# Layer 3's coupling: the first half kept as the input of its first Gelu, the last additions on three engines

## The chip, the cores and the metric

The kernel runs on one core of a Trainium2 chip. The metric is device time in microseconds of one execution of the whole program; the median of several executions is given with the lowest and the highest. Beside it stands one execution recorded by the hardware profiler, whose rows are used for everything inside the kernel.

The engines are named as in the profile: PE is TensorE (matmuls), PEld its weight loads, ACT is ScalarE, DVE is VectorE, POOL is GpSimd, SP the engine that issues the DMAs here.

## The reference, cut to what matters

The program runs four layers, each with an attention-like part and a feed-forward part. Only the end of the last layer is touched. There, a state x of 4096 rows by 128 features goes three times through a coupling. Its coefficient comes from a small net on x and from a context net on the mean of x:

```
for cycle in 0, 1, 2:
    h = gelu(x @ c1 + cb1)          # 128 -> 128
    h = gelu(h @ c2 + cb2)          # -> 64
    h = gelu(h @ c3 + cb3)          # -> 32
    c = base + c2s * tanh((h @ c4 + cb4) / 2)   # one number for each row
    x = x + c * twist(x)            # twist is a fixed signed permutation of features
out = residual + x
```

The lines are the mathematics as the kernel computes it: base comes from the context net and holds one number for each batch entry, c2s is a constant of the layer. The matrix twist, applied twice, gives minus the identity, so that several cycles together are a*x + b*twist(x) with two numbers a and b for each row.

## The kernel before, in words

The 4096 rows are eight blocks of 512. A block lies with its features on the partitions, as the tile xT[i] of 128 x 512; two batch entries of 256 rows make a block. Blocks 0 to 3 are the first half, 4 to 7 the second (HALVES). The residual lies with rows on the partitions, as X[i].

The first cycle's c1 of blocks 0 to 3 is done inside the last layer's attention, by attended (line 1285), where two single PSUM banks are to be had. After attention, bank gives one of four PSUM buffers, and tp has four more, named tw.

Each step of the coupling is a small function, and each works on one half. first (from line 1333) multiplies a block by c1 and runs the Gelu on ACT from PSUM (L1339). second joins two blocks in one bank (L1347), third joins four (L1355). fourth multiplies by c4 for each block; ACT's tanh (L1401) gives the coefficient, repeated over all 128 partitions; DVE multiplies it by the constant and the twisted block (L1402); POOL and DVE in turn add that to xT (L1403). twists makes the twisted block on PE, in tw, and lets DVE add the part of base at once (L1391, two instructions for each block). columns_of computes the same coefficients once more with rows on the partitions (cd on PE, L1362 on ACT, L1366 on DVE), and keeps the products a and b up.

In the last cycle xT of the first half is not updated. finish_first forms a*x + b*twist(x) from the tile with rows on the partitions, xn, for all four blocks: m is the b part (L1435), in four instructions for each block, y is scaled by a (L1436), and both are added to the residual (L1440, L1441). POOL makes m and y for blocks 0 and 1, DVE for blocks 2 and 3; DVE does all additions. The second half is different: rest_in (L1416) adds its xT to the residual through PE, turn_second twists it on PE (tx), and finish_second adds the twisted block times the coefficient (L1457), on DVE. SP then issues each output block's DMA.

The order of everything after attention is written out by hand under a manual schedule of PE, ACT, DVE and POOL: each engine runs its instructions in the order of the calls, and waits only for what an instruction reads and for the buffer that it writes to. The two halves alternate, so that PE works on one half while ACT and DVE are busy with the other.

Of the kernel before, what the change touches and what calls it, by code (L numbers as in the profile page):

```python
# [10 lines left out]
F32 = mybir.dt.float32  # L11
# [3 lines left out]
ALU = mybir.AluOpType  # L15
# [40 lines left out]
def program(ctx: ExitStack, tc: tile.TileContext, x, consts, consts0, rows, pk0, w0s, w0e, pk1, pk1i, pk2, pk3, out):  # L56
# [1201 lines left out]
    with tc.tile_pool(name="l3w", bufs=1) as wp:  # L1258
# [11 lines left out]
        with banks(2, 3), tc.tile_pool(name="l3a", bufs=2) as sp:  # L1270
            gx = wp.tile([P, B], F32, tag="gx", name="gx")

            def means():
                yield from norm_steps(fp, (NBLK - 1,), 3, kept)
                for i in range(NBLK):
                    nc.vector.tensor_reduce(
                        gx[:, 2 * i : 2 * i + 2], xT[i].rearrange("p (b s) -> p b s", b=2), AX.X, ALU.add
                    )
                    yield
                nc.vector.tensor_scalar(gx, gx, 1.0 / S, None, ALU.mult)  # L1280
                yield

            h1 = {}

            def attended(s, gap, cT):


                ahead = {(16, 5): (0, 1), (17, 0): (2,), (17, 1): (3,)}
                for i in ahead.get((s, gap), ()):
                    ps = bank(f"c1_{i}_0")  # L1290
                    mm(ps, W3["c1"], xT[i])
                    h1[i] = wp.tile([P, 512], F32, tag=f"c1_{i}", name=f"c1_{i}_0")
                    nc.scalar.activation(h1[i], ps, AF.Gelu, bias=W3["cb1"])  # L1293
                if s in (14, 15) and gap in (1, 2, 4):
                    i = (s - 14) * 3 + gap // 2
                    po = bank(f"po3_{i}")
                    for t in range(NT):
                        ts_ = slice(t * P, (t + 1) * P)
                        mm(po[:, ts_], cT[i][:, ts_], W3["wo"])
                    xf = X[i].rearrange("p t d -> p (t d)")  # L1300
                    nc.vector.tensor_tensor(xf, xf, po, ALU.add)

            cTs = attention(sp, wp, range(NBLK), W3, 3, means(), attended)

        with banks(4, 0), tc.tile_pool(name="l3t", bufs=4, space=PSUM, reuse_waits="tile") as tp, \
# [24 lines left out]
            def first(hf, cyc, ns):  # L1333
                for n in ns:
                    i = HALVES[hf][n]
                    ps = bank(f"c1_{i}_{cyc}")
                    mm(ps, W3["c1"], xT[i])
                    h1[i] = sp.tile([P, 512], F32, tag="c1", name=f"c1_{i}_{cyc}", bufs=8)
                    nc.scalar.activation(h1[i], ps, AF.Gelu, bias=W3["cb1"])  # L1339

            def second(hf, cyc):
                for p in range(2):
# [6 lines left out]
            def third(hf, cyc):  # L1349
                ps = bank(f"c3_{hf}_{cyc}")  # L1350
                for n in range(4):
                    r = slice(64 * (n % 2), 64 * (n % 2) + 64)
                    mm(ps[32 * n : 32 * n + 32], W3["c3"][r], h2[hf, n // 2][r])
                h3[hf] = sp.tile([P, 512], F32, tag="c3", name=f"c3_{hf}_{cyc}", bufs=3)
                nc.scalar.activation(h3[hf], ps, AF.Gelu, bias=W3["cb3"])  # L1355
# [28 lines left out]
            def twists(hf, cyc):  # L1384

                for n, i in enumerate(HALVES[hf]):
                    ps = tws[i] = tp.tile([P, 512], F32, tag="tw", name=f"tw_{i}_{cyc}")
                    mm(ps, C["twist"], xT[i])
                    for b in range(2):
                        v = slice(b * S, (b + 1) * S)  # L1390
                        nc.vector.scalar_tensor_tensor(  # L1391
                            xT[i][:, v], ps[:, v], base[:, 2 * i + b : 2 * i + b + 1], xT[i][:, v], ALU.mult, ALU.add
                        )

            def fourth(hf, cyc):
                for n, i in enumerate(HALVES[hf]):
                    r = slice(32 * n, 32 * n + 32)
                    ps = bank(f"c4_{i}_{cyc}")
                    mm(ps, W3["c4"][r], h3[hf][r])
                    c = sp.tile([P, 512], F32, tag="c4", name=f"c4_{i}_{cyc}", bufs=4)  # L1400
                    nc.scalar.activation(c, ps, AF.Tanh, bias=hb4, scale=0.5)  # L1401
                    nc.vector.scalar_tensor_tensor(c, c, c2, tws[i], ALU.mult, ALU.mult)  # L1402
                    (nc.gpsimd, nc.vector)[n % 2].tensor_tensor(xT[i], xT[i], c, ALU.add)  # L1403

            def rest_in():


                for i in HALVES[1]:
                    po = tp.tile([P, 512], F32, tag="tw", name=f"po3_{i}")
                    for t in range(NT):  # L1410
                        ts_ = slice(t * P, (t + 1) * P)
                        if i >= 6:
                            mm(po[:, ts_], cTs[i][:, ts_], W3["wo"], True, False)
                        mm(po[:, ts_], xT[i][:, ts_], ident, i < 6, True)
                    xf = X[i].rearrange("p t d -> p (t d)")
                    nc.vector.tensor_tensor(xf, xf, po, ALU.add)  # L1416
# [2 lines left out]

            def finish_first():  # L1420

                made = []
                a, b = turn[0]
                nb = sp.tile([P, 2, 2, 4], F32, tag="nb", name="nb")
                nc.vector.tensor_scalar(nb, b, -1.0, None, ALU.mult)

                for n in (0, 2, 1, 3):
                    i, eng = HALVES[0][n], (nc.gpsimd, nc.vector)[n // 2]
                    x, y = X[i], xn3[i]
                    wide = lambda v, k: col(v, n).unsqueeze(2).to_broadcast([P, NT, k])  # L1430
                    quarter = lambda v, k: v[:, :, 32 * k : 32 * k + 32]
                    m = sp.tile([P, NT, D], F32, tag="m", name=f"m_{i}", bufs=4)

                    for k, of, v in ((0, 2, b), (1, 3, nb), (2, 0, nb), (3, 1, b)):
                        eng.tensor_tensor(quarter(m, k), quarter(y, of), wide(v, 32), ALU.mult)  # L1435
                    eng.tensor_tensor(y, y, wide(a, D), ALU.mult)  # L1436
                    made.append((i, x, y, m))
                for k in (1, 3, 0, 2):
                    i, x, y, m = made[k]
                    nc.vector.tensor_tensor(x, x, y, ALU.add)  # L1440
                    nc.vector.tensor_tensor(x, x, m, ALU.add)  # L1441
                    nc.sync.dma_start(out=ov[i], in_=x)

            last = {}
# [8 lines left out]
            def finish_second():  # L1453
                for n, i in enumerate(HALVES[1]):
                    x = X[i]
                    for t in range(NT):
                        nc.vector.scalar_tensor_tensor(  # L1457
                            x[:, t], last[i][:, t * P : (t + 1) * P], col(turn[1][1], n)[:, t : t + 1], x[:, t],
                            ALU.mult, ALU.add,
                        )  # L1460
                    nc.sync.dma_start(out=ov[i], in_=x)

            engines = {mybir.EngineType.PE, mybir.EngineType.Activation, mybir.EngineType.DVE, mybir.EngineType.Pool}
            with tc.manual_schedule(engines=engines):
                context_net()
                second(0, 0)
                twists(0, 0)
                first(1, 0, range(0, 2))
                third(0, 0)
                first(1, 0, range(2, 4))  # L1470
                fourth(0, 0)
                second(1, 0)
                columns_of(0, 0)
                twists(1, 0)
                for cyc in (1, 2):

                    first(0, cyc, range(0, 2))
                    third(1, cyc - 1)
                    first(0, cyc, range(2, 4))
                    fourth(1, cyc - 1)  # L1480
                    second(0, cyc)
                    columns_of(1, cyc - 1)
                    if cyc == 1:
                        twists(0, cyc)
                    else:
                        rest_in()
                    first(1, cyc, range(0, 2))
                    third(0, cyc)
                    first(1, cyc, range(2, 4))
                    if cyc == 1:  # L1490
                        fourth(0, cyc)
                        second(1, cyc)
                        columns_of(0, cyc)
                        twists(1, cyc)
                    else:
                        columns_of(0, cyc)
                        second(1, cyc)
                        finish_first()
                turn_second()
                third(1, 2)  # L1500
                columns_of(1, 2)
                finish_second()


# [155 lines left out]
```

## Time and profile before

| | us |
|---|---|
| median of 3 executions | 1350.15 |
| lowest to highest | 1348.76 to 1353.18 |
| profiled execution | 1435.41 |
| its span | 1433.6 |
| mean granted TensorE clock in it | 0.94 |
| PE busy in it | 1267.3 |
| DVE busy in it | 774.9 |
| ACT busy in it | 561.4 |
| POOL busy in it | 344.8 |

The profiled execution took 85 us longer than the median execution; its rows are used for durations and order, and sums are made against its own span. The coupling takes about the last 100 us of the span. The times on rows are in us from the start of the span.

### The profile page before, as it was taken

What the parts mean: (1) busy time and instruction counts of PE and PEld (TensorE: products, weight loads), DVE (VectorE), ACT (ScalarE), POOL (GpSimd) and SP (SyncE); (2) the same over time, 40 slices, a digit from 0 to 9 for tenths busy, and PEclk for the clock granted to TensorE, in tenths of its full rate; (3) what the DMA queues carried; (4) which work ended last, traced back from release to release, by engine and by line L of the source; (5) the groups of instructions that cost most, each with busy time, mean ns of one, the idle gap of its engine ahead of it and who ended that gap; (6) DMA issues with size and microseconds to landing.
All of it is one profiled execution on the core that took longest, in us unless ns stands there. A gap on an engine that the chain in (4) does not pass through costs nothing.

```text
span 1433.6 us, 27549 instructions
## 1 busy us (share of the span) xinstructions
PE 1267.3 (88%) x11630; PEld 812.5 (57%) x11630; DVE 774.9 (54%) x1587; ACT 561.4 (39%) x868; POOL 344.8 (24%) x512
## 2 busy tenths in 40 slices
PE   3733699987889999999899999999998999999896
PEld 2512469975555566666545555455555666667434
DVE  7422254435756677767446433554337666567267
ACT  4400122323334544453334433444234555553552
POOL 2456100064312100001012211222112444434012
PEclk9656799998889999999999999999999999999998
DMA  6922575874100000000000000000000000000002
GB/s 195 306 88 74 154 238 170 245 208 149 53 13 16 11 2 3 2 2 2 1 0 0 1 0 0 1 1 0 0 0 2 2 2 2 2 2 2 2 1 59
DMA packets 66731, 72.12 MB, mean 50 GB/s; under 512 B 7344, under 2 KB 57008, under 8 KB 66096
## 3 DMA queue, kind: packets, MB, share of 16 engines
q1 hardware_dynamic: 61936, 60.62, 13.7%
q0 software_dynamic: 4240, 8.99, 2.0%
q8 instruction: 92, 1.51, 0.4%
q10 hardware_dynamic: 432, 0.75, 0.2%
q14 instruction: 31, 0.25, 0.1%
HBM read 52.45 MB, written 17.89 MB: 49 GB/s over the span
## 4 chain that ended last, share of the span: by engine, by line
PE 78%; DVE 12%; issue 6%; ACT 3%; another core or an unknown queue 1%; POOL 0%; DMA 0%; ACTq 0%; DVEq 0%; POOLq 0%
PE h L117 15%; PE sc L117 9%; PE se L117 7%; PE po L117 6%; PE av L117 5%; DVE M L952 4%; PE c L117 3%; PE sy L117 3%; PE sg L117 3%; PE mT L967 2%; PE su L117 2%; PE cv L117 2%; PE pq L117 2%; PE pk L117 2%; PE a L117 1%
## 5 line engine op out<-in xcount | busy, mean ns | idle before, releaser
L952 DVE TENSOR_REDUCE M<-sc 128x4 f32<-128x1024 f32 (+3 forms) x256 | 196.1, 819 | 107.6 <-PE sc L117 98.9
L117 PE MATMUL h<-h,pk 128*128 128x512 f32 x512 | 221.6, 592 | 0.0
L997 ACT ACTIVATE E<-se 128x1024 f32<-128x1024 f32 (+1 forms) x192 | 158.9, 880 | 77.3 <-PE se L117 76.9
L117 PEld LDWEIGHTS h<-h,pk 128*128 128x128 f32 x512 | 96.4, 190 | 117.2 <-issue 115.0
L1004 POOL TENSOR_SCALAR_AFFINE_SELECT E<-E 64x256 f32<-64x256 f32 x240 | 100.5, 419 | 140.5 <-ACT E L997 129.0
L117 PE MATMUL se<-Q,Km 32*128 32x256 f32 (+3 forms) x2048 | 124.0, 336 | 9.9 <-DVE M L952 6.6
L117 PE MATMUL sc<-Kp,Qm 32*128 32x256 f32 (+3 forms) x2048 | 124.3, 338 | 3.0 <-DVE M L952 1.5
L117 PEld LDWEIGHTS sc<-Kp,Qm 32*128 32x128 f32 x2048 | 94.3, 192 | 57.3 <-issue 30.7
L668 POOL DMA_INDIRECT yk<-YS,slots x64 | 61.8, 965 | 248.6 <-DMA we<-in_w0e 135.9
L117 PEld LDWEIGHTS se<-Q,Km 32*128 32x128 f32 x2048 | 88.8, 188 | 48.8 <-issue 34.9
L123 POOL TENSOR_TENSOR v_r<-mv,power 128x4 f32<-128x4 f32 (+1 forms) x23 | 5.2, 226 | 441.1 <-DVE mv L144 441.1
L1243 ACT ACTIVATE h<-h,pk 128x512 f32<-128x512 f32 x64 | 44.0, 687 | 140.8 <-PE h L117 140.7
L117 PE MATMUL cv<-toe,Z 128*32 128x128 f32 x512 | 38.1, 346 | 55.6 <-issue 49.6
L1253 DVE TENSOR_TENSOR x<-x,po 128x512 f32<-128x512 f32 x8 | 5.5, 688 | 139.2 <-PE po L117 139.2
L117 PE MATMUL av<-E,vals 128*32 128x256 f32 (+3 forms) x2048 | 77.2, 301 | 3.8 <-ACT c L1293 1.5
L1022 ACT COPY cu<-av 128x512 f32<-128x512 f32 x32 | 18.8, 586 | 143.5 <-PE av L117 130.3
L449 POOL DMA_INDIRECT XS<-xn,slots x64 | 62.1, 970 | 49.4 <-issue 34.4
L117 PEld LDWEIGHTS av<-E,vals 128*32 128x32 f32 x2048 | 52.7, 110 | 25.0 <-ACT c L1293 2.4
L117 PEld LDWEIGHTS cv<-toe,Z 128*32 128x32 f32 x512 | 23.9, 193 | 68.1 <-issue 61.7
L649 DVE TENSOR_TENSOR hs<-hs,su 128x512 f32<-128x512 f32 x40 | 27.5, 687 | 58.5 <-PE su L117 50.3
L148 DVE TENSOR_SCALAR xn<-x,mv,r 128x128 f32<-128x128 f32 x100 | 46.8, 532 | 14.2 <-POOL r L124 14.1
L117 PE MATMUL sy<-we,hs 128*128 128x128 f32 x320 | 44.2, 283 | 6.9 <-DVE hs L649 6.9
(303 smaller groups left out, 2239.8 us busy)
## 6 DMA issues: line engine op xcount, KB each, us to landing
toe<-kd SPq DMA_DIRECT2D x32, 512.0 KB
we<-in_w0e SPq DMA_DIRECT2D x40, 384.0 KB
xs<-XS SPq DMA_DIRECT2D x40, 128.0 KB
YS<-ys SPq DMA_DIRECT2D x40, 128.0 KB
pk<-in_pk SPq DMA_DIRECT2D x1, 3145.5 KB
XS<-Z SPq DMA_DIRECT2D x3, 1024.0 KB
x<-in_x SPq DMA_DIRECT2D x8, 256.0 KB
ycd<-yc SPq DMA_DIRECT2D x8, 256.0 KB
```

The source lines that it names most:

```text
L117: nc.tensor.matmul(o, l, r, start=start, stop=stop)
L148: nc.vector.tensor_scalar(dst[:, t, :], src[:, t, :], mv[:, at + t, 0:1], r[:, at + t : at + t + 1], ALU.subtract, ALU.mult,)
L449: d = nc.gpsimd.indirect_dma_start(out=XS[:, :], out_offset=at_rows(slots[:, hf, k, n : n + 1]), in_=xn[HALVES[hf][n // NT]][:, n % NT, :] ...
L649: nc.vector.tensor_tensor(h, h, pu, ALU.mult)
L668: nc.gpsimd.indirect_dma_start(out=y, out_offset=None, in_=YS[0 : FIRST * SLOTS, :] if hf == 0 else YS[:, :], in_offset=at_rows(slots[:, h ...
L952: nc.vector.tensor_reduce(dst, src, AX.X, ALU.max, negate=True)
L967: nc.tensor.transpose(ps[:, T, c * P : (c + 1) * P], negm[bl][:, c, T].rearrange("p g j k -> p (g j k)"), ident)
L997: nc.scalar.activation(E[:, 2 * n : 2 * n + 2, :], se[n][:, :, 0 : 2 * wide], AF.Exp, scale=ISQ)
L1004: nc.gpsimd.affine_select(out=d[r], in_=d[r], pattern=[[0, 2], [0, 2], [1, 64]], compare_op=ALU.is_ge, fill=0.0, base=0, channel_multiplie ...
L1022: nc.scalar.copy(cu, ps.rearrange("p (t q) -> p t q", t=2))
L1243: nc.scalar.activation(hn[:, c, :], ps, AF.Gelu, scale=W2[sn][:, c : c + 1])
L1253: nc.vector.tensor_tensor(xf, xf, po, ALU.add)
```

## The change

The first half no longer updates xT. What it keeps is u, the input of the first Gelu without its bias, that is x times c1; and v, which is twist(x) times c1. Adding c*twist(x) to x takes u to u + c*v (v is held with its sign turned, so that the code subtracts), and v to v + c*u by the same sign. Both are tiles of 128 x 512 in SBUF.

- attended copies the four c1 results from PSUM to SBUF (us) by DVE, and ACT's Gelu reads the copy. At one point it computes turned, the product of the twist matrix and c1, with one small matmul and a copy.
- turned_sums takes the place of twists(0, 0): four matmuls of xT with turned, and four copies to SBUF by DVE (v).
- on_sums takes the place of fourth for the first half in cycles 0 and 1. For each block ACT runs the tanh and then two Identity instructions of 128 x 256 that apply the constant and the base. DVE forms c*v and subtracts it from u. In cycle 0 POOL forms c*u, which turned_again later adds to v on DVE.
- first_again takes the place of first for the first half in cycles 1 and 2: Gelus alone, without matmuls. twists(0, 1) is gone.
- The order by hand changes: third(0), fourth(1) and columns_of(1) stand elsewhere, and rest_in is called for two blocks at a time with columns_of(0) between.
- finish_first gives blocks 0 and 1 wholly to POOL, additions and all. For blocks 2 and 3 DVE joins the scaling by a with the addition, in four instructions, and adds m in one.
- In finish_second block 4 goes to ACT (four Copy instructions with the coefficient as their scale) and POOL (one addition). DVE has the other three blocks.

```diff
@@ attended
-                    nc.scalar.activation(h1[i], ps, AF.Gelu, bias=W3["cb1"])
+                    us[i] = wp.tile([P, 512], F32, tag=f"u_{i}", name=f"u_{i}_0")
+                    nc.vector.tensor_copy(us[i], ps)
+                    nc.scalar.activation(h1[i], us[i], AF.Gelu, bias=W3["cb1"])
+                if (s, gap) == (16, 4):
+                    ps = bank("turned")
+                    mm(ps[:, 0:P], C["twist"], W3["c1"])
+                    nc.vector.tensor_copy(turned, ps[:, 0:P])
...
+            def first_again(cyc, ns):
+                for n in ns:
+                    i = HALVES[0][n]
+                    h1[i] = sp.tile([P, 512], F32, tag="c1", name=f"c1_{i}_{cyc}", bufs=8)
+                    nc.scalar.activation(h1[i], us[i], AF.Gelu, bias=W3["cb1"])
...
+            def turned_sums():
+
+                for i in HALVES[0]:
+                    ps = tp.tile([P, 512], F32, tag="tw", name=f"v_{i}_ps")
+                    mm(ps, turned, xT[i])
+                    tws[i] = sp.tile([P, 512], F32, tag="vn", name=f"v_{i}_0", bufs=4)
+                    nc.vector.tensor_copy(tws[i], ps)
+
+            def on_sums(cyc):
+
+                for n, i in enumerate(HALVES[0]):
+                    r = slice(32 * n, 32 * n + 32)
+                    ps = bank(f"c4_{i}_{cyc}")
+                    mm(ps, W3["c4"][r], h3[0][r])
+                    c = sp.tile([P, 512], F32, tag="c4u", name=f"c4_{i}_{cyc}", bufs=4)
+                    nc.scalar.activation(c, ps, AF.Tanh, bias=hb4, scale=0.5)
+                    for b in range(2):
+                        v = slice(b * S, (b + 1) * S)
+                        nc.scalar.activation(
+                            c[:, v], c[:, v], AF.Identity, bias=base[:, 2 * i + b : 2 * i + b + 1], scale=c2
+                        )
+                    u, v = us[i], tws[i]
+                    cv = sp.tile([P, 512], F32, tag="cv", name=f"cv_{i}_{cyc}", bufs=3)
+                    nc.vector.tensor_tensor(cv, c, v, ALU.mult)
+                    if cyc == 0:
+                        us[i] = sp.tile([P, 512], F32, tag="un", name=f"u_{i}_1", bufs=4)
+                    nc.vector.tensor_tensor(us[i], u, cv, ALU.subtract)
+                    if cyc == 0:
+                        cu = sp.tile([P, 512], F32, tag="cu", name=f"cu_{i}", bufs=4)
+                        nc.gpsimd.tensor_tensor(cu, c, u, ALU.mult)
+                        pending.append((v, cu))
+
+            pending = []
+
+            def turned_again():
+                while pending:
+                    v, cu = pending.pop(0)
+                    nc.vector.tensor_tensor(v, v, cu, ALU.add)
...
-                    eng.tensor_tensor(y, y, wide(a, D), ALU.mult)
-                    made.append((i, x, y, m))
-                for k in (1, 3, 0, 2):
-                    i, x, y, m = made[k]
-                    nc.vector.tensor_tensor(x, x, y, ALU.add)
-                    nc.vector.tensor_tensor(x, x, m, ALU.add)
+                    if eng is nc.gpsimd:
+                        eng.tensor_tensor(y, y, wide(a, D), ALU.mult)
+                        eng.tensor_tensor(x, x, y, ALU.add)
+                    else:
+                        for t in range(NT):
+                            eng.scalar_tensor_tensor(x[:, t], y[:, t], col(a, n)[:, t : t + 1], x[:, t], ALU.mult, ALU.add)
+                    eng.tensor_tensor(x, x, m, ALU.add)
                     nc.sync.dma_start(out=ov[i], in_=x)
...
@@ finish_second
+                    if n == 0:
+                        m = sp.tile([P, NT, D], F32, tag="m", name=f"m_{i}", bufs=4)
+                        for t in range(NT):
+                            nc.scalar.activation(
+                                m[:, t], last[i][:, t * P : (t + 1) * P], AF.Copy, scale=col(turn[1][1], n)[:, t : t + 1]
+                            )
+                        nc.gpsimd.tensor_tensor(x, x, m, ALU.add)
+                        nc.sync.dma_start(out=ov[i], in_=x)
+                        continue
...
                 context_net()
                 second(0, 0)
-                twists(0, 0)
+                turned_sums()
+                third(0, 0)
                 first(1, 0, range(0, 2))
-                third(0, 0)
+                on_sums(0)
                 first(1, 0, range(2, 4))
-                fourth(0, 0)
                 second(1, 0)
                 columns_of(0, 0)
                 twists(1, 0)
+                turned_again()
                 for cyc in (1, 2):
-                    first(0, cyc, range(0, 2))
+                    first_again(cyc, range(4))
                     third(1, cyc - 1)
-                    first(0, cyc, range(2, 4))
+                    second(0, cyc)
                     fourth(1, cyc - 1)
-                    second(0, cyc)
                     columns_of(1, cyc - 1)
-                    if cyc == 1:
-                        twists(0, cyc)
-                    else:
-                        rest_in()
+                    third(0, cyc)
+                    if cyc == 2:
+                        rest_in(HALVES[1][0:2])
+                        columns_of(0, cyc)
+                        rest_in(HALVES[1][2:4])
                     first(1, cyc, range(0, 2))
-                    third(0, cyc)
+                    if cyc == 1:
+                        on_sums(cyc)
                     first(1, cyc, range(2, 4))
+                    second(1, cyc)
                     if cyc == 1:
-                        fourth(0, cyc)
-                        second(1, cyc)
                         columns_of(0, cyc)
                         twists(1, cyc)
                     else:
-                        columns_of(0, cyc)
-                        second(1, cyc)
                         finish_first()
```

More of the change, by code (lines that the diff above doesn't have):

```diff
@@ L1271, in program @@
             gx = wp.tile([P, B], F32, tag="gx", name="gx")
+            turned = wp.tile([P, P], F32, tag="turned", name="turned")
             def means():
@@ L1281, in means @@
                 yield
-            h1 = {}
+            h1, us = {}, {}
             def attended(s, gap, cT):
@@ L1403, in fourth, with rest_in @@
                     (nc.gpsimd, nc.vector)[n % 2].tensor_tensor(xT[i], xT[i], c, ALU.add)
-            def rest_in():
-                for i in HALVES[1]:
+            def rest_in(blocks):
+                for i in blocks:
                     po = tp.tile([P, 512], F32, tag="tw", name=f"po3_{i}")
@@ L1420, in finish_first @@
             def finish_first():
-                made = []
                 a, b = turn[0]
@@ L1474, in program @@
                 twists(1, 0)
+                turned_again()
                 for cyc in (1, 2):
-                    first(0, cyc, range(0, 2))
+                    first_again(cyc, range(4))
                     third(1, cyc - 1)
-                    first(0, cyc, range(2, 4))
+                    second(0, cyc)
                     fourth(1, cyc - 1)
-                    second(0, cyc)
                     columns_of(1, cyc - 1)
-                    if cyc == 1:
-                        twists(0, cyc)
-                    else:
-                        rest_in()
-                    first(1, cyc, range(0, 2))
-                    third(0, cyc)
+                    third(0, cyc)
[3 more added lines that the diff above has]
+                        rest_in(HALVES[1][2:4])
+                    first(1, cyc, range(0, 2))
+                    if cyc == 1:
+                        on_sums(cyc)
                     first(1, cyc, range(2, 4))
+                    second(1, cyc)
                     if cyc == 1:
-                        fourth(0, cyc)
-                        second(1, cyc)
                         columns_of(0, cyc)
```

## The prediction

> **What bounds the kernel now.** I read the page first, for the engine that carries the span, then stretches of the last 100 us, then the groups there, then the chain of waits at the end. The chart orders by engine busy time and by the chain that ended last:
>
> ```profile
> PE 1267.3 (88%) x11630; PEld 812.5 (57%) x11630; DVE 774.9 (54%) x1587; ACT 561.4 (39%) x868; POOL 344.8 (24%) x512
> ...
> PE 78%; DVE 12%; issue 6%; ACT 3%; another core or an unknown queue 1%; POOL 0%; DMA 0%; ACTq 0%; DVEq 0%; POOLq 0%
> ```
>
> TensorE (PE) bounds the whole. The edit, however, touches only layer 3's coupling, from about 1333 us on, so the table by stretch of that part decides. Columns: stretch, length, then busy us of PE, PEld, DVE, ACT, POOL with instructions, and after them the granted clock.
>
> ```profile
> core 0: us, PE busy (x) PEld busy (x) DVE busy (x) ACT busy (x) POOL busy (x), PEclk, DMA share, GB/s
> ...
> 1352.80:1365.70 12.90, 12.90 (x49) 5.00 (x48) 7.31 (x13) 7.29 (x12) 2.55 (x2) 1.00 0.01 1
> 1365.70:1378.70 13.00, 13.00 (x49) 5.00 (x48) 8.74 (x17) 7.29 (x12) 2.55 (x2) 1.00 0.00 0
> ...
> 1420.10:1433.60 13.50, 0.60 (x6) 0.51 (x5) 9.76 (x27) 0.27 (x1) 0.00 (x0) 0.55 0.54 155
> ```
>
> A half-cycle of the coupling is solid PE, with ACT a little over half busy. After 1420 PE is done and VectorE (DVE) works alone, which the chain shows:
>
> ```profile
> 1413.85 1.67 DVE m L1435 x4
> ...
> 1425.53 0.20 DVE cc L1366 x2
> ...
> 1427.41 2.58 DVE x L1457 x10
> ```
>
> PE ends at 1420.70 and the second half's coefficients are out of ACT at 1421.06, but DVE is still in finish_first until 1425.5. So the end has two limits in turn: PE, then DVE. The prices (last number before the idle time is ns of one):
>
> ```profile
> L117 PE MATMUL c<-xT,pk 128*128 128x512 f32 x48 | 23.3, 607 | 0.0
> L1339 ACT ACTIVATE c<-c,pk 128x512 f32<-128x512 f32 x20 | 13.8, 688 | 26.0 <-PE c L117 26.0
> L1391 DVE SCALAR_TENSOR_TENSOR xT<-tw,base,xT 128x256 f32<-128x256 f32 x32 | 13.1, 474 | 3.8 <-PE tw L117 3.8
> L1402 DVE SCALAR_TENSOR_TENSOR c<-c,c,tw 128x512 f32<-128x512 f32 x16 | 11.2, 739 | 17.6 <-ACT c L1401 17.6
> L1403 DVE TENSOR_TENSOR xT<-xT,c 128x512 f32<-128x512 f32 x8 | 10.2, 1279 | 0.3
> L1403 POOL TENSOR_TENSOR xT<-xT,c 128x512 f32<-128x512 f32 x8 | 10.2, 1275 | 66.1 <-DVE c L1402 66.1
> L1457 DVE SCALAR_TENSOR_TENSOR x<-tx,cc,x 128x128 f32<-128x128 f32 x16 | 4.2, 342 | 0.0
> L1440 DVE TENSOR_TENSOR x<-x,xn 128x512 f32<-128x512 f32 x4 | 2.7, 683 | 0.0
> ```
>
> A 128x512 matmul runs as two passes that start 0.43 us apart, so it costs PE 0.86. By their starts, ACT instructions of 128x512 follow each other every 0.57 us, and L1457's every 0.257.
>
> **The change part by part.**
>
> *In attention.* Four c1 results are copied to SBUF by DVE: 4 x 0.68 (row L1416, also a PSUM read). DVE is busy only 0.78 of the 12.1 us from 1333.5, and the copy frees the PSUM bank that the av matmul waits for (it starts at 1337.32, after an ACT table load of 1.28 and a 0.69 Gelu) some 0.8 early. One extra matmul (turned), waiting for DVE's cx on PE, gives part of that back. Net -0.5 by the first c2.
>
> *PE's ledger.* Gone: the first half's c1 in two cycles (8 x 0.86 = 6.9) and its second twist (4 x 0.86 = 3.4); 10.3 us, with their PSUM traffic. The first twist stays as matmuls by turned, now behind c2 and ahead of c3. DVE trades 8 x 0.395 (start to start) for 4 copies of 0.6 there.
>
> *ACT's ledger.* In on_sums each of four blocks has a tanh and two Identity passes of 128x256 with two pointer operands. No such size is in the trace. The nearest row is
>
> ```profile
> L264 ACT ACTIVATE xn<-x,off,r 128x128 f32<-128x128 f32 x28 | 11.4, 499 | 0.0
> ```
>
> whose starts lie 0.385 apart. Adding 128 columns at 0.83 ns (the ACT copies L1022 of 512 columns and L638 of 256: 586 less 373 ns, by 256) gives 0.59 for one and 0.475 from start to start (estimates). Bounds: 0.4 (little over that row's spacing) and 0.54; I take 0.475. So a block costs 0.69 + 0.06 + 2 x 0.475 = 1.7, where 0.57 was spent, and four cost 6.6. On ACT's queue behind them stand the Gelus of c1_6 and c1_7, and PE's c2_11 waits for the last of these. Banks add waits: the four PSUM buffers hold the c4 results, so c1_6, c1_7 and c2_10 wait each for one tanh. From the first c4 matmul to c2_11: 1.1 + 6.6 + 2 x 0.57 + 0.2 = about 9.1 us, in which PE has work for 5.5. What follows in the cycle is 13.6 of PE (c2 0.9, cd 0.9, four twists 3.4, c3 0.95, two c2 1.8, four c4 2.0, cd 0.95, c3 0.95, two c1 1.7, rounded) plus 0.6 of waiting for POOL's and DVE's update of xT. One cycle is thus 23.3 us, against 25.9 now (first c4 of the first half at 1357.5, then 1383.4). The 10.3 removed shrink to this: the rest turns into waits for ACT.
>
> *Where it goes then.* The first c4 moves from 1357.5 to 1355.1 (c1_6 and c1_7, 1.7, now stand behind it, and the 0.5 from above); its twin to 1378.4, 5.0 early. In the last cycle the gain is handed back: c3, cd and the po matmuls (5.5, row from 1401.28 in the chain) all precede the second half's c1, and po waits for the update of xT. From the twin: 9.1 + 0.9 + 0.9 + 3.4 + 0.95 + 1.8 + 2.0 + 0.95 + 0.95 = 21.0, then po 5.5, cd 0.9 and 0.7 of waiting: 1406.5, where it stands now at 1406.6. Only the c3 and cd that had come after it are saved: PE would end at 1418.5, 2.2 early.
>
> *DVE and POOL in on_sums.* Two products of SBUF operands on DVE per block (0.68), in the first pass beside POOL's cu (1.27). The trace shows such pairs serialised: POOL's L1403 at 1373.28 to 1374.56, DVE's at 1373.83 to 1375.11, 1.28 where L1440 with POOL idle takes 0.68. The rule in "SBUF — State Buffer", Who interferes with whom, agrees. At about 2.3 per block, four end near 1366, 1 to 2 us ahead of the STTs of the second half's twists, so I cost this at nothing; at 3 per block it would surface by about 1.
>
> *The finish.* finish_first no longer puts 8 additions of 0.66 on DVE; blocks 0 and 1 go wholly to POOL, 2 x (4 x 0.41 + 1.05 + 2 x 1.27) = 10.5 us from about 1409, when a and b are there (1413.67 now), done before 1422. DVE's part is 2 x (1.67 + 4 x 0.34 + 0.68) = 7.4 and some 2 to 3 of waiting for POOL's port: about 1420 instead of 1425.5. Coefficients: PE 1418.5, +0.4 ACT, +0.4 DVE. Then DVE has 12 of L1457 at 0.257 = 3.1 instead of 4.2; it ends at 1423.4. Block 4 takes 4 ACT Copies (0.38 each) and one POOL addition (1.27), ready about 1423; SP issues its DMA first and those of 6 and 7 queue behind it, 0.4 apiece: last issue about 1424.3 against 1430.4. The number of DMAs is the same and what lies behind the last issue stays. Sum without clock effects: -6.1.
>
> *The clock.* The rule that speaks against this change. The row first:
>
> ```profile
> 1342.86:1346.27 3.41, 1.78 (x12) 1.04 (x14) 0.27 (x2) 1.39 (x4) 0.00 (x0) 1.00 0.00 0
> 1346.27:1349.68 3.41, 3.41 (x9) 0.94 (x6) 0.32 (x2) 1.33 (x2) 0.00 (x0) 0.50 0.01 2
> ```
>
> A stretch with PE at 52% was followed by half clock for 3.41 us. The rule ("TensorE: Matmul & The Clock Gate", Part 1) only asks for an idle window of about 3.4 us, free-running, and warns of idle gaps over about 3. By the rule's wording my two gaps of 2.7 us (about 1361.4 to 1364.1, 1384.7 to 1387.5) would cost nothing: -6.1. By the row, a window lying on such a gap is only 20 to 30% busy and the next is at half clock: each costs 1.7 us of PE, more where a second follows. I side with the row, at 2 us each on average, as the windows' place varies: -6.1 + 4 = about -2.
>
> **Sum.** The span of 1433.6 (profiled execution 1435.41) becomes about 1431.5 (1433.3). The profiled execution is 85 us longer than the median 1350.15, with the last 100 us alone concerned, so I carry over the difference and not a share: 1350.15 - 2.1 = 1348.0. About 0.3% (4 us) is what a measurement of this kernel can tell from no change.
>
> **The rivals.**
>
> *The clock stays up* (the gaps straddle windows, or PE is busier than I think). For: gaps under 3.41 us. Against: the row above. Then -6.1, with Identity at 0.4 another -1.2: 1343 to 1344.5.
>
> *ScalarE becomes the bound and PE stays cold.* Its place is the c2_11 wait in both cycles. Once at half clock, PE returns only after a full window, and the c4 and c1 waits of each cycle break windows up; each half window adds 1.7. Break-even is at 6.1 / 1.7 = 3.6 such windows. With Identity at 0.54 (8 more passes per cycle, 2 x 8 x 0.065 = +1.0) and five or six windows, -6.1 + 1.0 + 9.4 = +4.3: 1354.5. For: ACT then holds 17 of 23 us of a cycle. Against: behind c2_11 stand 13 us of PE work that fills windows.
>
> *The finish brings it all.* The coupling gives nothing at PE's end (POOL's lock late, or waits for banks larger), and DVE's relief alone remains: about -4 if the clock holds, or 0 after 4 us of half clock: 1346 to 1350.
>
> **How the numbers follow.** My forecast (-4 to +1) 0.45, with most of it inside 0.3%; clock up 0.27, faster; finish alone 0.13, split; PE cold 0.15, of which two thirds over the limit. Faster 0.37, within 0.42, slower 0.21. The range runs from 1343.0 to 1354.5; the forecast's own from 1346 to 1351.
>
> **What would show it.** Right: ACT the releaser of PE at c2_11, twice, with idle of 2 to 3 us; half clock just after at least one of these; the second half's c1 of the last cycle still near 1406 when undisturbed; DVE in the last stretch with no L1440 additions and ending within 5 us of PE. Wrong: no half clock there (faster), a DVE or POOL that PE waits for in on_sums, or a POOL finish that ends behind DVE's and holds SP's queue.

## The result, and the profile after

The changed kernel takes 1354.24 us (median of 20 executions, 1351.45 to 1358.08); the kernel before, on the same chip, 1348.93 (20 executions, 1347.44 to 1353.24). The ratio is 1.0038, with a 95% interval of 1.0031 to 1.0045: about 5 us slower. The prediction was 1348.0 with a range of 1343.0 to 1354.5, a gain of 2 us where there was a loss of 5.

The profiled execution took 1357.15 us, more than most. The length goes with the clock: of the 20 executions, those from 1351.4 to 1353.1 list a mean clock of 0.964 to 0.969, those from 1357.1 on 0.957. Much of what the profiled one has more lies ahead of the coupling: ACT's last table load, from which times are taken below, comes 4.9 us later than in the profile of e4, which is the same program up to there (1253.54 and 1248.64).

The two profiled executions differ by 83 us long before anything that was changed, between 60 and 530 us from their starts. So all times here are taken from one instruction: ACT's load of its table, near the end of attention (L1293 before, L1297 after), which is at 1335.28 us of the profile before and at 1253.54 of the one after.

| us after the table load | before | changed | e1, PE kept busy | e5, reordered, old finish |
|---|---|---|---|---|
| first tanh of the first half, cycle 0 | 23.41 | 20.31 | 20.31 | 20.31 |
| the same, cycle 1 | 49.36 | 49.89 | 44.03 | 42.68 |
| a, b and nb for finish_first | 78.57 | 81.16 | 72.03 | 69.05 |
| PE's end | 85.42 | 92.28 | 83.15 | 80.16 |
| DVE's first tx instruction | 90.49 | 93.94 | 84.79 | 80.84 |
| last DMA issue | 94.74 | 97.45 | 88.31 | 85.09 |
| end of the span | 98.34 | 101.91 | 92.72 | 88.70 |
| windows of half clock until PE's end | 1 | 7 | 1 | 1 |

The changed kernel is 3.1 us early at the first tanh and late by the second cycle. What lies between is in the stretches of its profile. Columns as before: stretch, length, busy us of PE, PEld, DVE, ACT and POOL, granted clock, DMA share and GB/s. The stretches are the 3.41 us in which the clock changes.

```profile
1277.34:1280.76 3.42, 1.15 (x5) 0.20 (x4) 3.31 (x3) 3.35 (x8) 3.42 (x3) 1.00 0.00 0
1280.76:1284.17 3.41, 2.79 (x6) 0.89 (x6) 3.38 (x4) 1.93 (x4) 1.77 (x2) 0.50 0.03 7
1284.17:1287.58 3.41, 3.41 (x11) 2.38 (x11) 1.29 (x4) 2.30 (x5) 0.00 (x0) 0.50 0.00 0
1287.58:1291.00 3.42, 3.42 (x6) 1.35 (x5) 1.75 (x4) 0.90 (x2) 0.00 (x0) 0.50 0.00 0
...
1297.82:1301.24 3.42, 3.42 (x10) 0.84 (x3) 3.35 (x5) 1.35 (x3) 2.07 (x2) 0.50 0.00 0
1308.06:1311.48 3.42, 1.10 (x6) 0.19 (x2) 2.79 (x5) 3.39 (x8) 0.00 (x0) 1.00 0.00 0
1311.48:1314.89 3.41, 3.41 (x11) 1.75 (x10) 0.31 (x1) 1.27 (x3) 0.00 (x0) 0.50 0.00 0
1314.89:1318.30 3.41, 3.41 (x6) 1.77 (x7) 1.67 (x7) 2.72 (x5) 0.00 (x0) 0.50 0.00 0
```

Where the kernel before shows PE at 12.90 of 12.90 and 1.00, here ACT fills the first stretch (3.35 of 3.42), PE has 1.15 of it, and then three windows pass at half clock. The second on_sums does the same with two, and one more stands between, with no gap ahead of it. The chain of waits of the changed kernel names the wait and what follows it:

```profile
1279.66 1.09 ACT c L1427 x2
1280.76 0.58 ACT c L1347
1281.38 2.54 PE c L117 x4
1283.92 1.80 PE cd L117 x8
1285.72 6.22 PE tw L117 x8
```

c2_11 waits for a Gelu queued behind the last Identity pair. After it cd takes 1.80 us where the kernel before needed 0.80, and the four twists 6.22, where 3.4 is their time at full clock. The table of waits puts the gap at 2.3 us, twice (total, times, longest):

```profile
PE c L117 <- ACT c L1347: 4.6, 2, 2.3
```

The groups of the changed part, by form:

```profile
L1427 ACT ACTIVATE c<-c,base,c 128x256 f32<-128x256 f32 x16 | 8.7, 592 | 0.3
...
L1493 DVE SCALAR_TENSOR_TENSOR x<-xn,a,x 128x128 f32<-128x128 f32 x8 | 7.6, 1009 | 0.0
...
L1519 DVE SCALAR_TENSOR_TENSOR x<-tx,cc,x 128x128 f32<-128x128 f32 x12 | 3.2, 342 | 0.0
```

The Identity pass takes 0.592 us, as estimated. The finish has a surprise: L1493 and L1519 are the same instruction on the same size, but L1493, whose tensors both lie in SBUF, takes three times as long as L1519, which reads one from PSUM. In the chain of the end it is the largest piece (1336.16 and 1343.30):

```profile
1336.16 4.25 DVE x L1493 x4
1340.44 0.78 DVE x L1494
1341.22 2.08 DVE m L1487 x4
1343.30 3.23 DVE x L1493 x4
1346.55 0.69 DVE x L1494
```

PE ends at 1345.82, and DVE is through finish_first at 1347.24.

### The profile page after: what moved, and what is told of

Same layout as the page of the kernel before. It is cut to its first block, busy times and chain, and to the rows that moved or that the text cites. A ratio compares the mean times of both kernels' runs of the same rounds, so it can differ in the third digit from the quotient of the medians.

```text
span 1355.4 us, 27516 instructions
## 1 busy us (share of the span) xinstructions
PE 1243.8 (92%) x11608; PEld 805.8 (59%) x11608; DVE 786.0 (58%) x1584; ACT 571.6 (42%) x888; POOL 355.7 (26%) x517
## 4 chain that ended last, share of the span: by engine, by line
PE 76%; DVE 13%; POOL 3%; issue 3%; ACT 3%; DMA 1%; SPq 0%; DVEq 0%; POOLq 0%; ACTq 0%
PE h L117 16%; PE sc L117 9%; PE se L117 7%; PE po L117 6%; PE av L117 5%; DVE M L952 4%; PE mT L967 3%; POOL XS L449 2%; PE sy L117 2%; PE sg L117 2%; PE su L117 2%; PE pk L117 2%; PE pq L117 2%; PE c L117 2%; PE a L117 2%
## 5 line engine op out<-in xcount | busy, mean ns | idle before, releaser
L117 PE MATMUL se<-Q,Km 32*128 32x256 f32 (+3 forms) x2048 | 118.8, 332 | 3.9 <-DVE M L952 2.4
L117 PEld LDWEIGHTS se<-Q,Km 32*128 32x128 f32 x2048 | 85.6, 186 | 40.8 <-issue 27.2
L449 POOL DMA_INDIRECT XS<-xn,slots x64 | 64.9, 1014 | 35.5 <-DVE slots L420 16.3
L967 PE MATMUL mT<-consts,negm 128*128 128x128 f32 x256 | 35.9, 286 | 13.3 <-DVE negm L956 13.3
L117 PE MATMUL pk<-xT,pk 128*128 128x512 f32 x80 | 44.4, 637 | 2.3 <-ACT Qm L885 2.3
L117 PE MATMUL pq<-xT,pk 128*128 128x512 f32 x80 | 44.7, 646 | 0.9 <-DVE x L1128 0.8
```

Source lines behind the costliest of these rows:

```text
L117: nc.tensor.matmul(o, l, r, start=start, stop=stop)
L449: d = nc.gpsimd.indirect_dma_start(out=XS[:, :], out_offset=at_rows(slots[:, hf, k, n : n + 1]), in_=xn[HALVES[hf][n // NT]][:, n % NT, :] ...
L967: nc.tensor.transpose(ps[:, T, c * P : (c + 1) * P], negm[bl][:, c, T].rearrange("p g j k -> p (g j k)"), ident)
```

## The experiments

The theories: (1) the loss is half clock after PE's gaps in on_sums; (2) it is the waiting for ScalarE itself; (3) it is the new finish. Ratios are against the kernel before, run beside each set.

**e1_fill.** PE's gaps are filled with matmuls that nobody reads.

```diff
+            def keep_busy(cyc, k):
+                ps = tp.tile([P, 512], F32, tag="tw", name=f"idle_{cyc}")
+                for _ in range(k):
+                    mm(ps[:, 0:S], C["twist"], xT[4][:, 0:S])
...
                 first(1, 0, range(2, 4))
+                keep_busy(0, 6)
                 second(1, 0)
```

(The same stands ahead of second(1, 1).)

> The changed kernel with six idle 128x256 matmuls on PE ahead of c2_10 in cycles 0 and 1, whose results nobody reads; they take 6 x 0.43 = 2.6 us of the 3.4 us that PE stands idle at the end of on_sums. Theory 1 (the loss is TensorE's half clock after those gaps: five windows of 3.41 us at half clock after them in the changed kernel's profile, 1.7 us of PE each): the windows after both on_sums stay at full clock, PE's end comes 5 to 8 us earlier, and the time is 5 to 8 us below the changed kernel's 1354.2: 1346 to 1349. Theory 2 (PE waits for ScalarE, and the clock only follows): filling the gap changes no wait, so the time stays within 1.5 us of 1354. Theory 3 (the loss lies in the finish, where DVE and POOL lock each other out): 1354 as well.

Measured: 1344.35 us, ratio 0.9969 (0.9960 to 0.9978). That is a little more than theory 1 said, and more work for PE made the kernel 0.7% faster than the changed one (0.9969 by 1.0038). The stretches around the first gap, which the changed kernel went through at 0.50:

```profile
1273.01:1276.43 3.42, 3.42 (x17) 2.20 (x15) 3.31 (x3) 3.35 (x8) 3.42 (x3) 1.00 0.00 0
1276.43:1279.84 3.41, 3.04 (x15) 1.57 (x14) 3.38 (x4) 2.53 (x5) 1.79 (x2) 1.00 0.01 2
```

ACT's and POOL's busy times in the first of them are those of the changed kernel, PE is busy, and the clock stays at 1.00. In the table the end of the span moves from 101.91 to 92.72: the six extra windows cost 9.2 us, 1.5 each.

**e2_order.** Useful work goes into the gap instead.

```diff
                 first(1, 0, range(2, 4))
-                second(1, 0)
                 columns_of(0, 0)
                 twists(1, 0)
+                second(1, 0)
                 turned_again()
```

(The same in cycle 1.)

> The changed kernel with columns_of(0) and twists(1) called ahead of second(1) in cycles 0 and 1: 0.9 + 3.4 us of work that PE has to do anyway goes into the gap, where c2_10 and c2_11 had stood. Theory 1: no half clock after on_sums, and PE's waiting is used besides, so 2 to 3 us a cycle more than filling alone, less 1 us for the third layer of the second half that now comes later: 1342 to 1347. Theory 2: the 2 to 3 us a cycle of waiting alone, 1349 to 1352. Theory 3: 1354.

Measured: 1342.26 us, ratio 0.9945 (0.9929 to 0.9960), and its span ends 89.72 us after the table load, 3.0 before e1. So theory 2 is true as well, but for 3.0 us where the clock has 9.2.

**e3_finish.** The kernel before with the new finish_first and finish_second alone.

> The kernel before with the new finish_first and finish_second alone. Theory 1: from PE's end to the last DMA issue it was 9.7 us before and 5.7 in the changed kernel, so 4 us below the kernel before: 1345. Theory 3: the new finish is what loses; no faster than before, 1349 or more.

Measured: 1350.50 us, ratio 1.0009 (0.9999 to 1.0019). In the trace its span ends 1.1 us later than before, at 99.45. The ratio alone does not tell it from no change. The 4 us that I expected were a misreading: PE had come late in the changed kernel, which made the time from PE's end look short. The line's own durations (min, median and max, in ns) show what the sharing does:

```profile
L1440 DVE SCALAR_TENSOR_TENSOR x<-xn,a,x x8: 337/1310/1420, 1330.5 to 1340.5; 128x128 f32<-128x128 f32 x8
```

Alone the instruction takes 337 ns. Beside POOL's additions of 1.26 us, each takes 1.42, since it starts beside one and ends just after it. So DVE's finish_first takes 12.9 us from nb to its last addition, where the old one took 11.85.

**e4_coupling.** The changed kernel with the old finish_first and finish_second.

> The changed kernel with the old finish_first and finish_second: the coupling's part alone. Theory 1: the 4 us of the finish are missing, 1358, and the half clock after both on_sums is there as before. Theory 3: below 1354, about 1349.

Measured: 1350.97 us, ratio 1.0015 (1.0001 to 1.0029). The trace has the seven windows of half clock, PE ends at 92.14 as in the changed kernel, and the span ends at 100.73, 1.2 before it. So theory 3 holds for about 1 us in the trace. Of that 0.3 is in the last issue and 0.8 after it: the new finish issues its last three DMAs of 256 KB within 1.0 us, while the old one had at least 1.03 us between any two. The executions put more between the two kernels: ratios of 1.0015 and 1.0038, about 3 us, and the intervals do not meet. What the other 2 us are is not shown.

**e5_oldfinish.** e2 with the old finish_first and finish_second.

> The reordered kernel (columns_of and twists ahead of second) with the old finish_first and finish_second. In the reordered kernel's trace the first half's a and b are there 69.0 us after ACT's table load and PE ends at 80.1. The old finish_first took 11.85 us from there: 80.9, no later than the second half's coefficients. If the new finish costs only what its trace shows (0.3 us at the last issue and 0.8 us of landing, after three DMAs issued within 1.4 us), this is 0 to 1 us below the reordered kernel: 1341 to 1342.5. If the port lock between DVE and POOL costs more, as the 3 us between the coupling alone (1351.0) and the whole change (1354.2) might say: about 1339.

Measured: 1339.43 us, ratio 0.9921 (0.9899 to 0.9943), with 6 executions. The trace has 88.70, 1.0 below e2, which is the first of the two expectations; the median is lower than that, but the two intervals overlap.

**e6_oldfirst.** e2 with the old finish_first and the new finish_second.

> The reordered kernel with the old finish_first and the new finish_second (block 4 by ACT and POOL, DVE 12 instead of 16 instructions at the end). If finish_first's lock is what the new finish pays, as fast as with both old, or 0.5 us faster by four STTs of 0.257 less: 1341. If the DMAs bunched at the end are, 0.8 us slower than with both old, as slow as the reordered kernel: 1342.3.

Measured: 1341.18 us, ratio 0.9925 (0.9902 to 0.9947); the median is not to be told from e5's. In the trace the last issue comes at 84.30, 0.8 before e5, and the end at 88.71, the same. What four instructions less on DVE gain is given back while the bunched DMAs land. The whole 1.0 us of e2's finish is thus finish_first's lock.

**e7_warmstart.** e5 with idle matmuls in the context net.

```diff
+                fill = tp.tile([P, 512], F32, tag="tw", name="idle")
+                mm(fill[:, 0:S], C["twist"], xT[4][:, 0:S])
                 ps = bank("gc1")
...
+                mm(fill[:, 0:P], C["twist"], xT[4][:, 0:P])
                 ps = bank("gc2")
```

(And one more ahead of gc3.)

> The reordered kernel with the old finish, and three idle matmuls between those of the context net (0.87 us in the gaps where PE waits for ACT). The one window of half clock that all kernels have so far, about 10 us after the table load, should go: PE's busy share in the window before was 0.51 to 0.59. By the clock theory 1.7 us below the kernel with the old finish alone, about 1340. If this window has another cause, no change.

Measured: 1340.61 us, ratio 0.9926 (0.9905 to 0.9947): no gain over e5. The trace says why. The window 10 us after the table load is gone, and the first tanh comes at 18.66 instead of 20.31. But two others appear, each after a stretch in which PE still waits for the c4 banks:

```profile
1270.20:1273.62 3.42, 2.28 (x11) 1.11 (x10) 3.06 (x3) 3.35 (x7) 2.99 (x2) 1.00 0.02 5
1273.62:1277.03 3.41, 3.41 (x7) 1.70 (x7) 3.31 (x3) 3.24 (x7) 3.41 (x3) 0.50 0.01 2
```

**e8_fillone.** e1 with the filling in cycle 0 alone.

> The changed kernel with the six idle matmuls in cycle 0 only. Clock theory: cycle 1's gap is left and brings two windows of half clock, which cost 1.7 us each where PE is the bound: 3 to 3.5 us above the kernel filled in both cycles, 1347.5 to 1348. If what counted in the filled kernel was something else than the windows after each gap, no such step: 1344 or 1354.

Measured: 1349.52 us, ratio 0.9997 (0.9983 to 1.0011), 22 executions from 1341.19 to 1354.44. The median is 5.2 above e1, where I had said 3 to 3.5. The profiled execution (1344.06) had no window of half clock until PE's end, although cycle 1's gap was there:

```profile
1296.02:1299.43 3.41, 2.21 (x6) 0.49 (x6) 2.79 (x5) 3.34 (x7) 0.00 (x0) 1.00 0.01 2
1299.43:1302.85 3.42, 1.64 (x5) 0.44 (x5) 2.26 (x4) 2.85 (x6) 0.00 (x0) 1.00 0.00 0
1302.85:1306.26 3.41, 3.41 (x15) 2.08 (x15) 2.00 (x9) 3.06 (x6) 0.00 (x0) 1.00 0.00 0
```

Here the gap lies across the edge of two windows (2.21 and 1.64 of 3.4), and the clock stays. In the changed kernel's profile it lay within one (1.10 of 3.42). PE ends at 81.49, 1.66 before e1, which is what the one window costs that is missing here and stands in e1 10 us after the table load. So where the clock stayed up, the gap left open cost no more than the gap filled.

The executions between 1341 and 1343 list a mean clock of 0.975 to 0.976 each, those at 1354 list 0.961 to 0.962. Not all of that spread is the gap's: in the profiles of the changed kernel and of e1 to e12 the table load, ahead of the coupling, comes anywhere from 1247.71 to 1253.54 us, and the kernel before, without such a gap, spread over 8.4 us in the 30 executions beside e9 to e12.

**e9_dve_c.** The changed kernel with the two Identity passes on DVE.

```diff
-                        nc.scalar.activation(
-                            c[:, v], c[:, v], AF.Identity, bias=base[:, 2 * i + b : 2 * i + b + 1], scale=c2
-                        )
+                        nc.vector.tensor_scalar(
+                            c[:, v], c[:, v], c2, base[:, 2 * i + b : 2 * i + b + 1], ALU.mult, ALU.add
+                        )
```

> The changed kernel with the two Identity passes of each block done by DVE as tensor_scalar instead of ACT. ACT's stretch in on_sums falls from 6.7 to 2.3 us, so PE's gap of 3.4 us before c2_11 closes. If ScalarE's share of the edit made the loss, through gap and clock, PE gets 3 us a cycle and the 9 us of half clock back, 1341 to 1345. If DVE takes its place as the bound (2.36 us a block beside POOL in cycle 0, and 0.5 to 0.6 more now), PE waits there instead and cools again: 1348 to 1353.

Measured: 1342.43 us, ratio 0.9957 (0.9941 to 0.9972). ScalarE's share of the edit is what opened the gaps. DVE takes less for it than I had allowed (mean ns of one):

```profile
L1427 DVE TENSOR_SCALAR c<-c,c,base 128x256 f32<-128x256 f32 x16 | 5.8, 406 | 5.9 <-ACT c L1424 5.9
```

PE ends at 81.83, with three windows of half clock instead of seven. DVE is close to becoming the bound: the first half's next Gelus now wait for its u (total, times, longest), and PE for them.

```profile
ACT c L1353 <- DVE u L1435: 6.3, 4, 2.3
```

**e10_warm.** e7 with one more idle matmul ahead of c1_6 and of c1_7.

```diff
+            def first_warm(cyc):
+                ps = tp.tile([P, 512], F32, tag="tw", name=f"idle_{cyc}")
+                for n in (2, 3):
+                    mm(ps[:, 0:S], C["twist"], xT[4][:, 0:S])
+                    first(1, cyc, (n,))
```

> The reordered kernel with the old finish and the idle matmuls in the context net, and one more idle 128x256 matmul ahead of c1_6 and of c1_7 in both cycles, where PE waits 0.57 us for a bank each. With the context net's filling alone, two windows of half clock came back after shares of 0.67 and 0.68. Clock theory: none is left, 3 us below that kernel's trace (end 90.1 us after the table load, then 87), 1337 to 1338. If what is left there is no longer the clock: 1340.

Measured: 1338.19 us, ratio 0.9928 (0.9909 to 0.9947), 6 executions. No window of half clock is left in the trace, and the span ends at 87.05, as expected. By its trace this is the shortest coupling of all, 11.3 us below before; by the ratios it is not to be told from e5.

**e11_beforefill.** The kernel before with e7's idle matmuls.

> The kernel before with three idle matmuls (0.87 us) between those of the context net, nothing else. Its one window of half clock in the coupling, 11 us after the table load, should go: 1.7 us of PE, which bounds from there to PE's end, but DVE's finish_first hangs on the same chain, so the whole 1.7: 1347.2. If the clock there costs nothing: 1349.

Measured: 1348.53 us, ratio 0.9990 (0.9981 to 1.0000). A miss: the window did not go away in the profiled execution, although the stretch before it was now 72% busy.

```profile
1260.48:1263.89 3.41, 2.47 (x16) 1.61 (x16) 0.35 (x1) 1.34 (x4) 0.00 (x0) 1.00 0.00 0
1263.89:1267.31 3.42, 3.42 (x9) 0.92 (x6) 0.41 (x2) 1.06 (x3) 0.00 (x0) 0.50 0.01 2
```

**e12_columns.** The kernel before with the changed order of the last cycle alone.

```diff
-                    if cyc == 1:
-                        twists(0, cyc)
-                    else:
-                        rest_in()
-                    first(1, cyc, range(0, 2))
-                    third(0, cyc)
-                    first(1, cyc, range(2, 4))
...
+                    else:
+                        third(0, cyc)
+                        rest_in(HALVES[1][0:2])
+                        columns_of(0, cyc)
+                        rest_in(HALVES[1][2:4])
+                        first(1, cyc, range(4))
+                        second(1, cyc)
+                        finish_first()
```

> The kernel before with the changed kernel's order of the last cycle alone: third(0), and columns_of(0) between two halves of rest_in, ahead of the second half's first layer. PE's work is the same; a and b for finish_first come about 5 us earlier (78.6 us after the table load now), so that DVE is through finish_first at PE's end and not 4.8 us after it. If the order, and not the sharing among engines, is what shortens the finish: 4 us less, 1345. If it takes the sharing: 1348 to 1349.

Measured: 1344.60 us, ratio 0.9974 (0.9964 to 0.9983). In the trace nb comes at 74.31 instead of 78.57, PE ends where it did (85.43), and the span ends at 94.02 instead of 98.34. Its chain of waits now goes from PE to the second half's coefficients and through L1457 alone, without a finish_first between:

```profile
1330.28 1.03 PE c L117 x8
...
1332.08 1.07 PE cd L117 x8
...
1333.22 0.28 ACT cc L1362
...
1333.86 1.38 DVE x L1457 x5
```

## Why the prediction was wrong

*The coupling at full clock: right.* e1 is the changed kernel with the clock held up, and it gives the terms of the sum. The block in on_sums was put at 1.7 us and its tanhs stand 1.70 apart. First c4 to c2_11 was put at 9.1 and took 8.7. A cycle was put at 23.3 and took 23.7 in e1 (20.31 to 44.03), against 25.9 before. PE's end was put 2.2 early and came 2.3 early. The clock-free sum was -6.1; e1's span ends 5.6 early. (Both are counted from the table load, which comes 0.6 late itself; against attention they are 1.7 and 5.0.) Three slips in the working change little: 0.385 and 0.107 make 0.49, not 0.475, and 0.50 was measured; four blocks of 1.7 are 6.8, not 6.6; 1357.5 less 1.7 and 0.5 is 1355.3, not 1355.1.

*Attention: right.* The first c2 was put 0.5 early. Against the last attention instructions the table load comes 0.6 late and c2 stands 1.4 nearer to it, so it is 0.8 early.

*The clock: the term that failed.* I had written "each costs 1.7 us of PE, more where a second follows ... at 2 us each on average": 4 us in all. In the changed kernel's profile the first gap was followed by three windows and by one more later, the second by two. The price of one was right (1.5 measured); their number was not. I had reasoned that the 13 us of PE work behind c2_11 would bring the clock back after one window. It took three, although PE is listed as busy for 2.79 of 3.41 us in the first and for all of the second. The listed time hides what that work was. The first of those 13 us are c2_11, whose weights are 128*64, half of the largest in the traces (128*128), and cd, whose records stream four columns each and are still listed with 287 ns:

```profile
L117 PE MATMUL c<-c,pk 128*64 128x512 f32 x48 | 15.7, 709 | 5.8 <-ACT c L1347 4.6 <-ACT c L1424 1.1
...
L117 PE MATMUL cd<-pk,c 128*128 128x4 f32 x48 | 7.9, 287 | 0.8 <-ACT c L1369 0.8
```

A count over the traces supports this. Give each matmul record the 0.43 us that 512 columns take (half of it for bf16), scaled by its columns and by the size of its weights as a share of 128*128. By this estimate the windows from 1277.34 on hold 0.91, 0.86, 0.93 and 1.76 us of full-size work, and the clock is back after the fourth, in which the twists run; those from 1308.06 on hold 0.70, 0.70 and 1.53, and it is back after the third. Over all windows from the first clock record to PE's end in the 14 traces, half clock follows 284 of the 288 that hold less than 1.05 us, 53 of the 72 between 1.05 and 1.3, and none of the 4989 that hold more. By the listed busy time they do not separate: of 4087 windows with PE busy for 3.3 us or more, half clock follows 59. The traces share most of their program, and no run was made to test this count.

With 9.2 in the place of 4, the sum is -6.1 + 9.2 = +3.1. The trace has +3.6 (101.91 less 98.34), the executions +5.3; what lies between these two is not accounted for. This was the second rival, "PE stays cold", at its own price of five or six windows, and I gave it 0.15; its further 1.0 for a slower Identity did not come. The row that I had (52% busy, then half clock once) came from one window that recovered at once; it spoke for the effect, and I had no row for its length. By the wording of the rule in the Trainium skill ("TensorE: Matmul & The Clock Gate", Part 1), gaps of 2.3 us within a window of 3.4 might have been free; they were not, so that siding with the row was right. That the window runs free, as the page says, agrees with the traces: in the changed kernel, e1, e2, e4 and e5, the same program up to there, the first window of half clock begins between 9.78 and 10.15 us after the table load, and the gap of cycle 1 fell within one window in the changed kernel and across two in e8.

*The finish: the sum was near, its reason wrong.* I had it that sharing the additions brings DVE's finish_first from 1425.5 to 1420. e3's trace shows that sharing costs 1.1, and e12's that the order of the last cycle alone takes 4.3 off. By difference, only about 2.4 of e1's 5.6 are left for the coupling itself, from which 10.3 us of matmuls were removed; that is near PE's end, 2.3 early. The order was in my sum, as the a and b that come at 1409 instead of 1413.67; with the old finish_first's 11.85 that gives 1420.9, nearly all of the gain, and I booked it to the sharing. The term mis-sized here is "some 2 to 3 of waiting for POOL's port": five of the eight STTs that I had priced at 0.34 took 1.20 to 1.43, 5.2 us more than priced. The rule that I cited for on_sums (the Trainium skill, "SBUF — State Buffer", Who interferes with whom) covers these too: two SBUF inputs on DVE beside a POOL instruction that reads SBUF. In on_sums its price held: DVE's work of the first pass took 9.4 us for four blocks, 2.36 each where I had 2.3, and stayed hidden.

*The rival "ScalarE becomes the bound".* ScalarE was the bound for 2.3 us, twice, plus the bank waits. e2 shows what that alone is worth, 3.0 us. It was the gap's effect on the clock and not the gap that decided the sign.

*What stays open.* What exactly makes a window count as idle. PE's busy share does not tell it: 0.32 and 0.34 brought half clock, but so did 0.67 (e7) and 0.72 (e11), while 0.48 and 0.65 did not (e8). The count of full-size work puts e7's windows at 1.13 and 1.09 us, e11's at 0.91 and e8's second gap window at 0.86; the last is one of its four exceptions, so that it is not settled why e8's clock stayed up. Between 1.05 and 1.3 the count does not decide either: there lies the stretch ahead of the changed kernel's window from 1297.82, with 1.21 us, although PE is listed as busy throughout.

## What to carry to other kernels

When an edit moves work off the engine that bounds a stage, ask how idle that engine becomes at the worst place, not only what it saves: here 10.3 us of matmuls were removed, and half clock, most of it after two gaps of 2.3 us, cost 9.2. Ask also what follows the gap: by the count above, matmuls of few columns or with small weights did not bring the clock back. Such a gap is best filled with later work of the same engine by changing the order of calls (e2, e5), or else with idle matmuls (e1, e10). And before an end is shared among engines, see whether its input can come earlier: the order of the last cycle was worth 4.3 us in the traces, and sharing the additions cost 1.1.

## What the runs showed of the hardware that was not expected

Return from half clock can be slow: in the changed kernel three windows in a row (10.2 us), the first two with PE 82% and 100% busy by the listed time. In the kernel before it took one. The two held 0.86 and 0.93 us of full-size work, the kernel before's held 1.70 (estimates, by the count above).

A DVE instruction of 128x128 with two SBUF inputs took 0.34 us alone and 1.42 beside POOL additions of 1.26: four small instructions each paid for a whole large one.

Output DMAs of 256 KB that were issued 0.5 us apart ended no earlier than those issued 1.03 us apart (e6 and e5: last issue 84.30 and 85.09, end 88.71 and 88.70).
